# A conditioned two-matmul block on one core: the first LayerNorm, its shift and scale and the first weight loaded and applied in halves

## The chip, the cores and the metric

The kernel runs on one core of one Trainium2 chip. A core has a matrix engine (PE), a vector engine (DVE), a scalar engine (ACT), a general engine (POOL) and a queue engine (SP) that here only issues DMAs. Each engine works through its own list of instructions in order; they wait for one another by semaphores. The metric is the device time of one execution in microseconds (us), the median over runs.

## The reference

`x` is (2, 2048, 512) in float32, `t` (the condition) is (2, 512). All weights are float32.

```python
emb = jnp.dot(jax.nn.silu(t), ada_w) + ada_b
shift_msa, scale_msa, gate_msa, shift_mlp, scale_mlp, gate_mlp = jnp.split(emb, 6, axis=-1)
norm = _ln(x) * (1.0 + scale_msa[:, None]) + shift_msa[:, None]
h = jax.nn.gelu(jnp.dot(norm, ssm_w1) + ssm_b1, approximate=False)
ssm_out = jnp.dot(h, ssm_w2) + ssm_b2
x = x + gate_msa[:, None] * ssm_out
norm2 = _ln(x) * (1.0 + scale_mlp[:, None]) + shift_mlp[:, None]
hf = jax.nn.gelu(jnp.dot(norm2, ff_w1) + ff_b1, approximate=True)
ff_out = jnp.dot(hf, ff_w2) + ff_b2
x = x + gate_mlp[:, None] * ff_out
```

`_ln` is a LayerNorm without weights over the last axis. `ssm_w1` and `ssm_w2` are 512x512, `ff_w1` is 512x1024, `ff_w2` 1024x512. `ada_w` is 512x3072: six blocks of 512 columns, called groups 0 to 5 (0 and 1 are shift and scale of the first LayerNorm, 2 its gate, 3 and 4 shift and scale of the second, 5 its gate).

## The kernel before

The 4096 rows are cut into eight blocks of 512 rows. For each block four matrix stages run: `hA_i` (first LayerNorm's output times w1, GELU), `oA_i` (times w2, added to x), `hC_i` (second LayerNorm's output times ff_w1, GELU) and `oC_i` (times ff_w2, added to x). The order of all instructions is written out by hand: the program text is the order on every engine, and `hook` lists attach other engines' or later stages' work to a place "after product Pn" of a stage.

**Seven products.** A stage multiplies 2x2 quarters of its operands with seven products P1 to P7 instead of eight. `group` (L405) issues them on PE; each is four float32 matmuls of a 128x128 weight by 256 columns, and stands in the trace as eight records. The sums of quarters that the products need are made by other engines: those of the weight (`w_s`, by POOL, L340) and those of the activations (`nS` for a LayerNorm's output, `hSA` for a hidden stage's, by DVE, L340 too). The products accumulate in PSUM banks of three names, `y` (P1, then P6, P7, P4 on top of it), `x` (P2) and `v` (P5, then P3). So before P6 is added onto a bank `y`, an engine must have read what P1 left there; P7 waits in the same way for the reading of P6, P4 for that of P7, and P3 for that of P5.

In a hidden stage (`hidden`, L573) `after` reads the banks: P1, P6 and P5 are taken with the bias added (`take_first`: DVE, L594, or ACT in two halves if `on_act`, L592), P2, P7 and P3 are added to what was taken (DVE, L600, L607, L610) and pass through the GELU on ACT (L601, L608, L611); P4 goes through ACT alone (L614). In a residual stage (`residual`, L628) each product is added to x by DVE (L642).

**The first stages.** The rows of `t` and of the biases come by four small DMAs on ACT's queue. On SP's queue follow, in this order: x of block 0 (two halves), groups 0 and 1 of `ada_w`, w1, group 2, w2, the biases of the gate, b2, x of block 1, groups 3 and 4, ff_w1, group 5, ff_w2 and more. PE passes its first microseconds with matmuls of an identity that nobody reads (`idle`, L803), among them one that turns the rows (`rowsT`). DVE makes the statistics of the four 128-row slots of block 0 (`stats`, L454 and L455, one `mv` each), then copies the turned rows (`colsT`, L808), and ACT makes `silu` of them (L811). POOL and DVE turn the statistics into a scale and an offset per row (`scales`, L463 to L474; POOL's share is an addition and a power). ACT and DVE apply them (`normal`, L494 and L498, two slots each), PE turns the result (`pt`, L523, sixteen transposes in four banks), and ACT and DVE apply scale and shift per column while they move it from PSUM to SBUF (`modulate`, L537 and L539), which yields `nT`, the operand of `hA_0`.

Shift and scale come from `modulation(g0, part)`: `rows_of(g)` multiplies `silu` with a group of `ada_w` (`pada`, L267, sixteen small matmuls, 32 records), DVE turns the result (L283) and adds the bias (L287). The gate's rows come from `gate_rows_of` (the same matmuls, DVE L295), and `first_ssm_gate` spreads them over 128 partitions with four matmuls (`pgate`, L302). DVE then multiplies b2 with the gate (`gb`, L855) and folds the gate into the four parts of w2 (L388). POOL adds the product `gb` to x (`biases`, L654, four instructions) and makes the four sums of the folded w2 (`w_s`, L340).

Before the change the order of `hA_0` is P1, P2, group 2's rows, P5, `pgate`, P6, P3, P7, group 3's rows (`modulation(3, 0)`), P4. That of `oA_0` is P1, P2, P5, P6, group 4's rows (`modulation(3, 1)`), P7, P3, eight transposes of block 1, P4, eight more. DVE takes P1, P5 and P6 of `hA_0`.

Of the kernel before, what the change touches and what calls it, by code (L numbers as in the profile page):

```python
# [36 lines left out]
F32 = mybir.dt.float32  # L37
AF = mybir.ActivationFunctionType
ALU = mybir.AluOpType
# [101 lines left out]
def kernel(  # L141
# [52 lines left out]
    def big_tile(name):  # L194
        return big.tile([P, KD, D], F32, tag="big", name=name)
# [11 lines left out]
    def load_ada(g):  # L207
        ada[g] = big_tile(f"ada_{g}")
        nc.sync.dma_start(
            out=ada[g], in_=ada_w[:, g * D : (g + 1) * D].rearrange("(k p) n -> p k n", p=P)  # L210
        )

    def load_w(name, w, t=None, eng=nc.sync):
        if t is None:
            t = const.tile([P, w.shape[0] // P, w.shape[1]], F32, tag=name, name=name)
        eng.dma_start(out=t, in_=w.rearrange("(k p) n -> p k n", p=P))
        return t
# [16 lines left out]
    load_ada(0)  # L234
    load_ada(1)
    w1_sb = load_w("w1", w1)
# [22 lines left out]
    mods = {}  # L259
# [17 lines left out]

    def modulation(g0, part):

        g = g0 + part  # L280
        pa = rows_of(g)
        turned = pa[:, P : 2 * P]
        nc.vector.transpose(turned, pa[:, :P])  # L283
        turned = turned.rearrange("p (n q) -> p n q", n=KD)
        m = const.tile([P, KD, B], F32, tag=f"mod_{g0}_{part}", name=f"mod_{g0}_{part}")
        bias = colsT[:, R_ADA + g * KD : R_ADA + (g + 1) * KD]
        nc.vector.tensor_tensor(m, turned[:, :, :B], bias.unsqueeze(2).to_broadcast([P, KD, B]), ALU.add)  # L287
        mods[g0, part] = m

    gate, gate_rows = {}, {}  # L290
# [150 lines left out]
    class Norm:  # L441
# [40 lines left out]

        def blocks(self):
            return work.tile([P, C, KD, C, Q], F32, tag="blocks", name=f"blocks{self.name}")

        def normal(self, c, eng=None, on_pe=False):

            if c == 0:
                self.nT = big_tile(f"nT{self.name}")
                self.xn = self.blocks().rearrange("p m k c q -> p m (k c q)") if on_pe else self.nT  # L490
# [178 lines left out]
    hA_0 = forms[:, :8].rearrange("p n a r -> p (n a r)").rearrange("p (k t) -> p k t", k=KD)  # L669
# [137 lines left out]
    run(n1[0].stats())  # L807
    nc.vector.tensor_copy(colsT, pt[:, :ROWS])  # L808

# [5 lines left out]
    )  # L815

    for g in (1, 4):
        rows_g = colsT[:, R_ADA + g * KD : R_ADA + (g + 1) * KD]
        nc.vector.tensor_scalar(rows_g, rows_g, 1.0, None, ALU.add)

# [4 lines left out]
    n1[0].scales(on_dve=True)  # L825

    w1_ops, w1_sums, _ = weight_of_first("w1", w1_sb)
    run(w1_sums)
    modulation(0, 0)
    for c in range(C):  # L830
        n1[0].normal(c, nc.vector if c % 2 else None, on_pe=True)
    modulation(0, 1)
    pts = {}

    def transposed(k):
        pts[k] = n1[0].transpose(k, ps_g.tile([P, TB], F32, tag="yv"[k % 2], name=f"pt1_0_{k}"))

    for k in range(KD):
        transposed(k)
    for k in range(KD):  # L840
        n1[0].modulate(k, pts[k], nc.vector if k % 2 else None)
# [20 lines left out]
    hook(hooks, ("P2",), [lambda: gate_rows_of(2, "grows")] + n1_sums[3:])  # L862
    st = n1[1].stats()
    hook(hooks, ("P5",), [ssm_gate, gb2_0] + biases(0, b2_bc) + fold2(0, 1))
    hook(hooks, ("P6",), fold2(1, 7))
    hook(hooks, ("P3", "P7"), st[:2])
    hook(hooks, ("P7",), [lambda: modulation(3, 0)])
    hA[0] = First(0, n1[0].ops, hooks, ("P1", "P2", "P5", "P6", "P3", "P7", "P4"), hA_0)
# [7 lines left out]
    hook(hooks, ("P6",), [lambda: modulation(3, 1)])  # L876
    hook(hooks, ("P3", "P3", "P4"), n1[1].turned())
    n2 = {0: Norm(0, 2)}
# [268 lines left out]
```

## Time and profile before

| what | us |
|---|---|
| median of 5 runs | 597.76 |
| the five runs | 599.62, 597.76, 597.59, 597.76, 599.25 |
| the profiled execution, its own time | 599.62 |
| its span, first to last instruction | 597.8 |
| PE, DVE, ACT, POOL busy in it | 589.9, 373.0, 220.3, 394.2 |
| mean granted PE clock | 0.996 of full speed |

The profiled execution is the slowest of the five. The page gives busy times and the waits of each engine; the chain of waits follows the work that ended last back from the end; a table by stretches gives busy times and the clock that was granted to PE; the timeline lists the instructions of an engine in order of time, with start, duration, engine, line, operation, the tile written and the tiles read, and in brackets how long the engine sat idle before and what released it. "PEld" is PE's loading of weights, beside its matmuls.

### The profile page before, as it was taken

What the parts mean: (1) busy time and instruction counts of PE and PEld (TensorE: products, weight loads), DVE (VectorE), ACT (ScalarE), POOL (GpSimd) and SP (SyncE); (2) the same over time, 40 slices, a digit from 0 to 9 for tenths busy, and PEclk for the clock granted to TensorE, in tenths of its full rate; (3) what the DMA queues carried; (4) which work ended last, traced back from release to release, by engine and by line L of the source; (5) the groups of instructions that cost most, each with busy time, mean ns of one, the idle gap of its engine ahead of it and who ended that gap; (6) DMA issues with size and microseconds to landing.
All of it is one profiled execution on the core that took longest, in us unless ns stands there. A gap on an engine that the chain in (4) does not pass through costs nothing.

```text
span 597.8 us, 8294 instructions
## 1 busy us (share of the span) xinstructions
PE 589.9 (99%) x2875; PEld 511.7 (86%) x2875; DVE 373.0 (62%) x637; ACT 220.3 (37%) x366; POOL 394.2 (66%) x465
## 2 busy tenths in 40 slices
PE   7999999999999999999999999999999999999997
PEld 4888888888888888888888888888888888888886
DVE  4879898997654475655754458653665236468642
ACT  2234337305532264233721356232553234212410
POOL 1678489999943995549968499966974696440200
PEclk9999999999999999999999999999999999999999
DMA  8990322300223104350052601331030400021001
GB/s 317 396 377 4 89 63 80 107 36 35 63 80 106 53 1 107 135 146 1 15 145 66 208 9 42 100 72 70 1 70 2 115 27 2 0 67 76 1 1 71
DMA packets 23702, 50.13 MB, mean 84 GB/s; under 512 B 4544, under 2 KB 5100, under 8 KB 22764
## 3 DMA queue, kind: packets, MB, share of 16 engines
q1 hardware_dynamic: 20624, 45.38, 23.8%
q10 hardware_dynamic: 3036, 4.22, 3.0%
q8 instruction: 23, 0.38, 0.3%
q14 instruction: 19, 0.16, 0.1%
HBM read 26.51 MB, written 8.40 MB: 58 GB/s over the span
## 4 chain that ended last, share of the span: by engine, by line
PE 97%; DMA 2%; DVE 1%; SPq 0%; issue 0%
PE py_oC L420 18%; PE px_hC L741 10%; PE py_oA L420 9%; PE pv_oC L420 9%; PE py_hA L420 9%; PE py_hC L741 8%; PE pv_hC L741 8%; PE pv_oA L420 5%; PE px_oC L420 5%; PE pv_hA L420 4%; PE py_hC L420 2%; PE px_oA L420 2%; PE px_hA L420 2%; DMA ada<-in_L_cond_ada_w_dram 2%; PE pv_hC L420 1%; PE pt L523 1%
## 5 line engine op out<-in xcount | busy, mean ns | idle before, releaser
L654 POOL TENSOR_TENSOR x<-x,gb 128x512 f32<-128x512 f32 x64 | 79.4, 1272 | 7.8 <-issue 4.6
L537 ACT ACTIVATE nT<-nT,mod,mod 128x512 f32<-128x512 f32 x54 | 39.6, 802 | 102.4 <-DMA nT<-blocks 96.2
L463 POOL TENSOR_SCALAR ve<-mv 128x4 f32<-128x4 f32 x16 | 3.7, 230 | 92.3 <-DVE mv L455 85.5
L494 ACT ACTIVATE nT<-x,nmr,rstd 128x512 f32<-128x512 f32 x56 | 42.4, 803 | 52.9 <-POOL nmr L481 37.1
L420 PE MATMUL py_oC<-fw,hClo 128*128 128x256 f32 x256 | 57.9, 379 | 0.0
L420 PEld LDWEIGHTS py_oC<-fw,hClo 128*128 128x128 f32 x256 | 48.6, 190 | 6.6
L642 DVE TENSOR_TENSOR x<-py_oC,x 128x512 f32<-128x512 f32 (+1 forms) x36 | 22.6, 630 | 42.9 <-PE py_oC L420 42.9
L454 DVE BATCH_NORM_STATS2 st<-x 128x6 f32<-128x512 f32 x64 | 43.5, 679 | 5.1 <-DMA x<-in_x_dram 4.8
L340 POOL TENSOR_TENSOR hSC<-hClo,hChi 128x512 f32<-128x512 f32 (+1 forms) x17 | 20.1, 1187 | 39.9 <-ACT hChi L736 29.2
L741 PE MATMUL py_hC<-forms,fw 128*128 128x256 f32 x168 | 40.8, 379 | 0.0
L758 DVE TENSOR_TENSOR hClo<-hClo,py_hC 128x512 f32<-128x512 f32 x42 | 28.4, 681 | 16.9 <-ACT hClo L755 10.4
L505 DVE STREAM_TRANSPOSE blocks<-nT 128x512 f32<-128x512 f32 x56 | 37.8, 694 | 1.3 <-ACT nT L494 0.9
L679 POOL TENSOR_TENSOR forms<-forms 128x256 f32<-128x256 f32 x48 | 35.5, 740 | 2.8
L741 PEld LDWEIGHTS py_hC<-forms,fw 128*128 128x128 f32 x168 | 31.8, 190 | 4.4
L758 DVE TENSOR_TENSOR hChi<-hChi,pv_hC 128x512 f32<-128x512 f32 x35 | 23.3, 684 | 17.1 <-PE pv_hC L741 14.3
L642 DVE TENSOR_TENSOR x<-py_oA,x 128x512 f32<-128x512 f32 x32 | 22.0, 688 | 18.9 <-PE py_oA L420 18.3
L420 PE MATMUL py_hA<-nT,w 128*128 128x256 f32 x128 | 30.4, 380 | 0.0
L736 ACT ACTIVATE hClo<-hClo,colsT 128x256 f32<-128x256 f32 x56 | 25.4, 500 | 10.8 <-DVE hClo L758 10.7
L420 PE MATMUL py_oC<-fw_s,hSC 128*128 128x256 f32 x128 | 28.9, 379 | 0.0
L420 PE MATMUL pv_oC<-fw,hSC 128*128 128x256 f32 x128 | 28.9, 379 | 0.0
L420 PE MATMUL px_oC<-fw,hChi 128*128 128x256 f32 x128 | 28.9, 379 | 0.0
L420 PE MATMUL pv_oC<-fw_s,hSC 128*128 128x256 f32 x128 | 28.9, 379 | 0.0
(213 smaller groups left out, 1426.1 us busy)
## 6 DMA issues: line engine op xcount, KB each, us to landing
nT<-blocks SPq DMA_DIRECT2D x168, 64.0 KB
out_dram<-x SPq DMA_DIRECT2D x15, 512.0 KB
x<-in_x_dram SPq DMA_DIRECT2D x7, 1024.0 KB
ada<-in_L_cond_ada_w_dram SPq DMA_DIRECT2D x6, 1024.0 KB
fw<-in_L_cond_ff_w_dram SPq DMA_DIRECT2D x3, 2048.0 KB
nT<-blocks ACTq DMA_DIRECT2D x56, 64.0 KB
w<-in_L_cond_ssm_w_dram SPq DMA_DIRECT2D x3, 1024.0 KB
x<-in_x_dram SPq DMA_DIRECT2D x2, 512.0 KB
```

The lines of the kernel that those rows point to most:

```text
L340: eng.tensor_tensor(out[:, r], a[:, r], b[:, r], f)
L420: nc.tensor.matmul(ps[b][j * apart][:, j, :], lhs(p, j, k), rhs(p, j, k), start=(fresh and j * (not apart) == 0 and k == 0), stop=(p in (" ...
L454: nc.vector.bn_stats(st, xs[self.i][:, c, :])
L494: nc.scalar.activation(t, x_c, AF.Identity, bias=self.nmr[:, c : c + 1], scale=self.rstd[:, c : c + 1])
L505: nc.vector.transpose(self.bl[:, :, :, c, :].rearrange("p m k q -> p k m q"), self.nT[:, c, :].rearrange("p (k m q) -> p k m q", k=KD, m=C),)
L537: nc.scalar.activation(dst, src, AF.Identity, bias=shift, scale=scale)
L642: nc.vector.tensor_tensor(d, ps[BANK[p]][:, js], d, ALU.add)
L654: lambda c=c: nc.gpsimd.tensor_tensor(xs[i][:, c, :], xs[i][:, c, :], gb, ALU.add)
L679: eng.tensor_tensor(reg[d], reg[a], reg[b], ALU.add if f == "+" else ALU.subtract)
L736: nc.scalar.activation(h, h, AF.Gelu_apprx_tanh, bias=fb1T[:, m : m + 1])
L741: nc.tensor.matmul(ps[b][:, j, :], fa[ra][:, j * P : (j + 1) * P], fb[rb].rearrange("p a (c q) -> p c a q", q=Q), start=(fresh and j == 0) ...
L758: nc.vector.tensor_tensor(dest(d), dest(d), ps[b], op)
```

## The change

Shift and scale (groups 0 and 1) and w1 are loaded in two halves of their columns each, in the order shift low, scale low, shift high, scale high, w1 low, w1 high: six DMAs with rows of 1 KB where there were three with rows of 2 KB. `modulation` works on one half at a time and gives back its DVE part as a function (`finish`). The scales of the first LayerNorm are made for slots 0 and 1 and for slots 2 and 3 apart (`scales_of`); ACT normalizes slots 0 and 1, DVE slots 2 and 3. The transposes come as slots 0 and 1 of all four banks, then slots 2 and 3, between the rows of the low and the high halves. `nT` of block 0 lies in the second half of `forms` instead of a tile of the pool `big`.

In `hA_0` ACT takes P1, P5 and P6 (`on_act=True`), and the order is P1, P2, P5, group 2's rows, P6, `pgate`, P7, P3, P4. In `oA_0` group 3's rows stand between P6 and P7, and group 4's after P4 and the last transposes. The four statistics of block 1 (`st`) stand after P3, P4 of `hA_0` and, as before, after P1 of `oA_0`; `picks` is made later.

```diff
@@ -204,10 +204,12 @@
 
     ada = {}
 
-    def load_ada(g):
-        ada[g] = big_tile(f"ada_{g}")
+    def load_ada(g, half=None):
+        if not half:
+            ada[g] = big_tile(f"ada_{g}")
+        c = slice(0, D) if half is None else slice(half * D // 2, (half + 1) * D // 2)
         nc.sync.dma_start(
-            out=ada[g], in_=ada_w[:, g * D : (g + 1) * D].rearrange("(k p) n -> p k n", p=P)
+            out=ada[g][:, :, c], in_=ada_w[:, g * D : (g + 1) * D][:, c].rearrange("(k p) n -> p k n", p=P)
         )
 
     def load_w(name, w, t=None, eng=nc.sync):
@@ -231,9 +233,12 @@
     ident = const.tile([P, P], F32, tag="ident", name="ident")
     make_identity(nc, ident)
     load_x(0, 2)
-    load_ada(0)
-    load_ada(1)
-    w1_sb = load_w("w1", w1)
+    for half in range(2):
+        load_ada(0, half)
+        load_ada(1, half)
+    w1_sb = const.tile([P, KD, D], F32, tag="w1", name="w1")
+    for c in (slice(0, D // 2), slice(D // 2, D)):
+        nc.sync.dma_start(out=w1_sb[:, :, c], in_=w1[:, c].rearrange("(k p) n -> p k n", p=P))
     load_ada(2)
 
     nc.gpsimd.memset(brows[:, :2, :P], 0.0)
@@ -256,7 +261,45 @@
     load_ada(4)
     fw1_sb = load_w("fw1", fw1)
 
-    mods = {}
+    mods, pada = {}, {}
+
+    def modulation(g0, part, half=None):
+
+
+        g = g0 + part
+        if not half:
+            pada[g] = ps_g.tile([P, D], F32, tag="x", name=f"pada_{g}")
+            mods[g0, part] = const.tile([P, KD, B], F32, tag=f"mod_{g0}_{part}", name=f"mod_{g0}_{part}")
+        n = slice(0, KD) if half is None else slice(half * KD // 2, (half + 1) * KD // 2)
+        pa = pada[g][:, n.start * G : n.stop * G]
+        w = ada[g].rearrange("p k (n m q) -> p k m n q", n=KD, q=G)
+        for k in range(KD):
+            for m in range(P // G):
+                nc.tensor.matmul(
+                    pa[m * G : (m + 1) * G, :],
+                    silu[:, k, :],
+                    w[:, k, m, n],
+                    start=(k == 0),
+                    stop=(k == KD - 1),
+                    tile_position=(0, m * G),
+                    skip_group_check=True,
+                )
+        turned = pada[g][:, P + n.start * G : P + n.stop * G]
+        bias = colsT[:, R_ADA + g * KD : R_ADA + (g + 1) * KD][:, n]
+
+        def finish():
+            nc.vector.transpose(turned, pa)
+            to = mods[g0, part][:, n]
+            by_n = turned.rearrange("p (n q) -> p n q", q=G)
+            nc.vector.tensor_tensor(
+                to, by_n[:, :, :B], bias.unsqueeze(2).to_broadcast([P, n.stop - n.start, B]), ALU.add
+            )
+
+        if half is not None:
+            return finish
+        finish()
+
+    gate, gate_rows = {}, {}
 
     def rows_of(g):
 
@@ -274,20 +317,6 @@
                     skip_group_check=True,
                 )
         return pa
-
-    def modulation(g0, part):
-
-        g = g0 + part
-        pa = rows_of(g)
-        turned = pa[:, P : 2 * P]
-        nc.vector.transpose(turned, pa[:, :P])
-        turned = turned.rearrange("p (n q) -> p n q", n=KD)
-        m = const.tile([P, KD, B], F32, tag=f"mod_{g0}_{part}", name=f"mod_{g0}_{part}")
-        bias = colsT[:, R_ADA + g * KD : R_ADA + (g + 1) * KD]
-        nc.vector.tensor_tensor(m, turned[:, :, :B], bias.unsqueeze(2).to_broadcast([P, KD, B]), ALU.add)
-        mods[g0, part] = m
-
-    gate, gate_rows = {}, {}
 
     def gate_rows_of(g, tag):
         pa = rows_of(g)
@@ -480,13 +509,33 @@
             v.tensor_tensor(self.nmr, self.mv[:, :, 0], self.rstd, ALU.mult)
             v.tensor_scalar(self.nmr, self.nmr, -1.0, None, ALU.mult)
 
+        def scales_of(self, s):
+
+            n, v = f"{self.name}_{s.start}", nc.vector
+            if s.start == 0:
+                self.rstd = small.tile([P, C], F32, tag="rstd", name=f"rstd{self.name}")
+                self.nmr = small.tile([P, C], F32, tag="nmr", name=f"nmr{self.name}")
+            ve, r, e = [small.tile([P, C], F32, tag=k, name=f"{k}{n}")[:, s] for k in ("ve", "r", "e")]
+            nc.gpsimd.tensor_scalar(ve, self.mv[:, s, 1], EPS, None, ALU.add)
+            nc.gpsimd.tensor_tensor(r, ve, minus_half[:, s], ALU.pow)
+
+            def rest():
+                v.tensor_tensor(e, r, ve, ALU.mult)
+                v.scalar_tensor_tensor(e, e, -0.5, r, ALU.mult, ALU.mult)
+                v.scalar_tensor_tensor(self.rstd[:, s], e, 1.5, r, ALU.add, ALU.mult)
+                v.scalar_tensor_tensor(
+                    self.nmr[:, s], self.mv[:, s, 0], -1.0, self.rstd[:, s], ALU.mult, ALU.mult
+                )
+
+            return rest
+
         def blocks(self):
             return work.tile([P, C, KD, C, Q], F32, tag="blocks", name=f"blocks{self.name}")
 
         def normal(self, c, eng=None, on_pe=False):
 
             if c == 0:
-                self.nT = big_tile(f"nT{self.name}")
+                self.nT = nT_0 if self.name == "1_0" else big_tile(f"nT{self.name}")
                 self.xn = self.blocks().rearrange("p m k c q -> p m (k c q)") if on_pe else self.nT
             t = self.xn[:, c, :]
             x_c = xs[self.i][:, c, :]
@@ -666,7 +715,10 @@
 
     forms = const.tile([P, 16, C, HT // C], F32, tag="forms", name="forms")
 
-    hA_0 = forms[:, :8].rearrange("p n a r -> p (n a r)").rearrange("p (k t) -> p k t", k=KD)
+    hA_0, nT_0 = [
+        forms[:, n : n + 8].rearrange("p n a r -> p (n a r)").rearrange("p (k t) -> p k t", k=KD)
+        for n in (0, 8)
+    ]
 
     def sums_of_registers(program, reg, engs):
 
@@ -804,8 +856,14 @@
             idle, ident, ident.unsqueeze(1).to_broadcast([P, C, P]), start=True, stop=True
         )
 
-    run(n1[0].stats())
+    halves = slice(0, C // 2), slice(C // 2, C)
+    st = n1[0].stats()
+    run(st[:2])
+    scales_lo = n1[0].scales_of(halves[0])
+    run(st[2:])
     nc.vector.tensor_copy(colsT, pt[:, :ROWS])
+    scales_hi = n1[0].scales_of(halves[1])
+    scales_lo()
 
 
     nc.scalar.activation(
@@ -813,32 +871,42 @@
         colsT[:, R_COND:R_ADA].rearrange("p (b k) -> p b k", b=B),
         AF.Silu,
     )
+    for c in (0, 1):
+        n1[0].normal(c, on_pe=True)
 
     for g in (1, 4):
         rows_g = colsT[:, R_ADA + g * KD : R_ADA + (g + 1) * KD]
         nc.vector.tensor_scalar(rows_g, rows_g, 1.0, None, ALU.add)
+    scales_hi()
+    for c in (2, 3):
+        n1[0].normal(c, nc.vector, on_pe=True)
+    w1_ops, w1_sums, _ = weight_of_first("w1", w1_sb)
+    run(w1_sums)
+
+
+    pts = {k: ps_g.tile([P, TB], F32, tag="yv"[k % 2], name=f"pt1_0_{k}") for k in range(KD)}
+
+    def transposed(k, slots):
+        for c in slots:
+            nc.tensor.transpose(pts[k][:, c * P : (c + 1) * P], n1[0].xn[:, c, k * P : (k + 1) * P], ident)
+
+    for finish in [modulation(0, part, 0) for part in range(2)]:
+        finish()
+    for k in range(KD):
+        transposed(k, (0, 1))
+    for k in range(KD):
+        transposed(k, (2, 3))
+    n1[0].modulate(0, pts[0])
+    n1[0].modulate(1, pts[1], nc.vector)
 
     picks = const.tile([P, P // G, P], F32, tag="picks", name="picks")
     nc.vector.tensor_copy(
         picks, ident.rearrange("p (m q) -> p m q", q=G)[:, :, :1].to_broadcast([P, P // G, P])
     )
-    n1[0].scales(on_dve=True)
-
-    w1_ops, w1_sums, _ = weight_of_first("w1", w1_sb)
-    run(w1_sums)
-    modulation(0, 0)
-    for c in range(C):
-        n1[0].normal(c, nc.vector if c % 2 else None, on_pe=True)
-    modulation(0, 1)
-    pts = {}
-
-    def transposed(k):
-        pts[k] = n1[0].transpose(k, ps_g.tile([P, TB], F32, tag="yv"[k % 2], name=f"pt1_0_{k}"))
-
-    for k in range(KD):
-        transposed(k)
-    for k in range(KD):
-        n1[0].modulate(k, pts[k], nc.vector if k % 2 else None)
+    for finish in [modulation(0, part, 1) for part in range(2)]:
+        finish()
+    n1[0].modulate(2, pts[2])
+    n1[0].modulate(3, pts[3], nc.vector)
     n1_sums = n1[0].summed(nc.vector)
     run(n1_sums[:2])
     load_ada(5)
@@ -859,13 +927,13 @@
 
     hooks = {}
     hook(hooks, ("P1",), n1_sums[2:3])
-    hook(hooks, ("P2",), [lambda: gate_rows_of(2, "grows")] + n1_sums[3:])
+    hook(hooks, ("P2",), n1_sums[3:])
     st = n1[1].stats()
-    hook(hooks, ("P5",), [ssm_gate, gb2_0] + biases(0, b2_bc) + fold2(0, 1))
-    hook(hooks, ("P6",), fold2(1, 7))
-    hook(hooks, ("P3", "P7"), st[:2])
-    hook(hooks, ("P7",), [lambda: modulation(3, 0)])
-    hA[0] = First(0, n1[0].ops, hooks, ("P1", "P2", "P5", "P6", "P3", "P7", "P4"), hA_0)
+    hook(hooks, ("P5",), [lambda: gate_rows_of(2, "grows")])
+    hook(hooks, ("P6",), [ssm_gate, gb2_0] + biases(0, b2_bc) + fold2(0, 1))
+    hook(hooks, ("P7",), fold2(1, 7))
+    hook(hooks, ("P3", "P4"), st[:2])
+    hA[0] = First(0, n1[0].ops, hooks, FIRST, hA_0, on_act=True)
     w2_ops = found["w2"][0]
 
     hA_sums = hA[0].summed(nc.vector)
@@ -873,8 +941,9 @@
     hooks = {}
     hook(hooks, ("P1",), hA_sums[2:3] + st[2:] + [n1[1].scales] + fold2(7, 8))
     hook(hooks, ("P2",), hA_sums[3:] + [lambda c=c: n1[1].normal(c, on_pe=True) for c in range(C)])
-    hook(hooks, ("P6",), [lambda: modulation(3, 1)])
+    hook(hooks, ("P6",), [lambda: modulation(3, 0)])
     hook(hooks, ("P3", "P3", "P4"), n1[1].turned())
+    hook(hooks, ("P4",), [lambda: modulation(3, 1)])
     n2 = {0: Norm(0, 2)}
     st = n2[0].stats()
     hook(hooks, ("P3",), st[:2])
```

## The prediction

> **What bounds the kernel now.** The page first: its busy times, and the shares of the chain that ended last.
>
> ```profile
> PE 589.9 (99%) x2875; PEld 511.7 (86%) x2875; DVE 373.0 (62%) x637; ACT 220.3 (37%) x366; POOL 394.2 (66%) x465
> PE 97%; DMA 2%; DVE 1%; SPq 0%; issue 0%
> ```
>
> PE is the bound. The change leaves the number of products alone, so it can only gain where PE waits or runs slowly. The chain in order of time (start, length, what) shows where that is:
>
> ```profile
> 2.11 9.84 DMA ada<-in_L_cond_ada_w_dram
> 11.99 1.58 PE pada L267 x32
> 13.57 3.01 PE pt L523 x16
> 16.58 1.73 PE py_hA L420 x8
> ```
>
> Until 11.99 us the end is set by the loads of shift and scale; from the first product of `hA_0` (first matmul at 16.42) PE goes from product to product at 1.73 each. What stands ahead of 16.42 can be shortened, nothing else. Then the table by stretches (length, busy time of each engine, granted PE clock, DMA):
>
> ```profile
> 5.59:9.00 3.41, 2.80 (x7) 0.81 (x5) 3.14 (x11) 0.22 (x1) 0.62 (x2) 1.00 1.03 385
> 9.00:12.42 3.42, 1.51 (x48) 1.27 (x52) 1.98 (x8) 1.52 (x2) 0.80 (x1) 1.00 1.04 390
> 12.42:15.83 3.41, 3.41 (x35) 3.03 (x28) 0.81 (x3) 0.78 (x1) 1.10 (x1) 0.50 1.04 387
> 31.00:40.00 9.00, 9.00 (x71) 7.68 (x69) 8.79 (x15) 0.84 (x2) 5.06 (x9) 1.00 1.04 389
> ```
>
> Two readings. After a stretch of 3.4 us in which PE was busy for 1.51, the clock was 0.50 for the next 3.41: sixteen transposes took 3.01 where eight take 0.87 in the chain at 43.87, and `pada` 1.58 instead of 1.08. That is 1.27 + 0.50 = 1.8 us of this execution, and the five times lie in two groups just so far apart (597.6 to 597.8; 599.25 and 599.62). The profiled one, 599.62, paid it; the median run, 1.86 below, did not. And from 31 to 40 us DVE is busy 8.79 of 9.00: beside PE there is no slack in `oA_0`. Its timeline, with PE's and POOL's lines:
>
> ```profile
> 31.15 1.27 POOL L340 TENSOR_TENSOR w_s<-w,w_s 128x512 f32<-128x512 f32 x1
> 31.40 1.57 DVE L340 TENSOR_TENSOR hSA<-forms 128x512 f32<-128x512 f32 x1
> 32.38 1.72 POOL L340 TENSOR_TENSOR w<-w 128x512 f32<-128x512 f32 x1
> 33.01 1.64 DVE L340 TENSOR_TENSOR hSA<-hSA,forms 128x512 f32<-128x512 f32 x1
> 37.32 1.89 PE L420 MATMUL py_oA<-w_s,hSA 128*128 128x256 f32 x8
> 37.95 0.68 DVE L340 TENSOR_TENSOR hSA<-forms,hSA 128x512 f32<-128x512 f32 x1
> 39.14 1.08 PE L267 MATMUL pada<-ada,silu 128*32 128x128 f32 x32
> 39.24 0.69 DVE L642 TENSOR_TENSOR x<-py_oA,x 128x512 f32<-128x512 f32 x1
> 40.15 1.99 PE L420 MATMUL py_oA<-w,forms 128*128 128x256 f32 x8
> ```
>
> DVE's addition of P6 ends at 39.93, group 4's rows cover that time on PE, and P7, which reuses P6's bank, starts at 40.15. It just fits. A sum `hSA` costs 0.68 alone and 1.6 while POOL makes sums of its own.
>
> **The change, part by part (us).**
>
> *Loads.* 1 MB of `ada_w` takes 2.65 (9.37 to 11.99; group 0 thus begins near 6.7). The halves have rows of 1 KB. The trace's packets of 1,024 bytes, the closing stores, took 48 ns, those of 2,048 bytes 88 at 9 to 15 us: two for one is 1.09 times as long, 1.46 a half. Landings: shift low 8.15, scale low 9.6, shift high 11.1, scale high 12.55, w1 low 14.0, w1 high 15.45. Bounds: no loss (w1 low 13.4) and 1 KB slowed as 2 KB was at 5.5 us, 97 for 88 (14.6). Three more DMAs cost SP three issues of 0.4 to 0.6, under loads already queued. Everything behind w1 lands some 0.8 later: w2 near 21.7 for its first use after 24, block 1's x near 25 for statistics at 28.5. Free; without that cover, 0.8.
>
> *LayerNorm in halves.* Statistics of slots 0 and 1 end at 6.47; POOL's 0.25 + 1.18 is done at 8.0. DVE's four small operations (0.20 each) follow `colsT` (8.29): 9.1. ACT's two normals (0.76 each) end at 9.9 and 10.65. The second half: POOL 8.29 to 9.8, DVE to 10.65, two normals of 0.5 to 11.6. Before, the last ended at 12.14.
>
> *PE until P1.* `silu` stays at 8.61. Half a group is 16 matmuls of 64 columns: between half of 1.08 and all of it; I take 0.87, since 32 weight loads alone took 0.81. Low halves 8.65 to 9.5 and 9.6 to 10.5; eight transposes (0.87) 10.7 to 11.55; eight more from 11.65 to 12.5; high halves to 13.4 and 14.25. Low shift and scale are ready at 12.4, the two modulations (0.8) at 13.3; the high ones at 14.85 and 15.65, before P2's turn at 16.0. So P1 starts at 14.25 (w1 low: 14.05) instead of 16.42: -2.17. Of this 1.8 is the slow clock that PE, now hardly idle, should avoid; against the median run only some 0.35 is left. Bounds: 13.6 (cheap half groups, full-rate loads) to 14.9.
>
> *ACT takes P1, P5 and P6.* DVE loses three operations of 0.60 spacing, ACT gains three of 0.84 (L614's pair) and has room (0.84 busy in nine). P6 stands ahead of `pgate` (1.04), which hides ACT's reading of it from P7, up to 0.1; uncovered 1.0.
>
> *Group 2's rows and `pgate` one product later.* Here the gain is given back. From P1 to the end of `pgate`: four products 6.92, rows 1.2 (19.93 to 21.13 with both gaps), `pgate` 1.04: 9.2, so DVE's `gb` starts at P1 + 9.4, 23.7. Before it was P1 + 7.6. The DVE work freed lies ahead of this wait and doesn't help. From there to the end of P6's addition in `oA_0`, by starts: `gb` 0.6, first fold 0.6, wait for P7 0.6, its addition 0.6, three folds 1.8, P3's addition 0.6, two statistics 1.6, two `hSA` 3.2, addition 0.6, sum 0.6, two statistics 1.6, P2's addition, `hSA`, P5's addition 1.8, P6's 0.7: 14.9, end at 38.6. PE from P1 to P7 of `oA_0`: eleven products 19.0, rows 2 x 1.2, `pgate` 1.04, the 0.1: 22.55, at 36.8. P7 must wait for the bank: 1.8; with 0.05 of signalling +1.85. Bounds: if the two `hSA` miss POOL's sums they cost 1.8 less and the stall is nil; if the sum behind them is caught too (POOL's three begin at 29.4, DVE's at 30.1), +0.5.
>
> *Groups 3 and 4.* The same 1.2 each, later; that group 3's rows left `hA_0` is in PE's sum above. DVE's part of group 4 (0.5) comes ahead of block 1's sums, ready at 49.4 for a product at 50.3. Nothing.
>
> *Sum* against the profiled execution's own time: 599.62 - 2.17 + 1.85 = **599.3**. This is 0.26% above the median before, whose runs had the first 1.8 already. A measurement can tell 0.3% from no change, here 1.8 us.
>
> [...] The row first: 1.51 busy of 3.42, with gaps of 0.4 and 1.54, was followed by half clock. [...]
>
> **The rivals.**
>
> *A, the forecast* (599.3; own range 598.6 to 600.0).
>
> *B, the stall brings the slow clock.* PE at P7 of `oA_0` is idle for 1.85, so a stretch of 3.41 that holds it whole has PE busy 1.56, like the 1.51 above; 2.80 kept the clock. If so the next 3.41 run at half: + 1.7, 601.0, slower than before. It decides where the stall lies wholly in one stretch: (3.41 - 1.85) / 3.41, 46% of the positions, which seem to shift from run to run. Against it: the least busy time that keeps the clock lies anywhere between 1.51 and 2.80.
>
> *C, no stall.* DVE gets by POOL, and P7 doesn't wait: 599.62 - 2.17 = 597.45, with an early P1 596.8. For it: three operations fewer on DVE. Against it: the wait for `pgate` comes after them.
>
> *D, the halves don't land earlier.* Rows of 1 KB need 60 ns or the slow clock falls on the transposes as before: P1 at 15.9, 599.62 - 0.5 + 1.85 = 601.0. Against it: 48 ns in the records, and gaps of 0.2 where there were 1.54.
>
> **How the numbers follow.** A 0.45, B 0.19, C 0.28, D 0.08. Before's median is 597.76, so "within 0.3%" is 595.97 to 599.55. Faster: a part of C, 0.11. Same: the rest of C and two thirds of A, 0.48. Slower: a third of A, B and D, 0.41. The predicted time is A's, 599.3; the range reaches from C's early end to B, 596.9 to 601.1.
>
> **What would show it.** Right: P1's first matmul at 14.0 to 14.6; clock 1.00 from 9 to 16 us; ACT with three pairs on L641; a gap of some 1.9 on PE ahead of the third `py_oA` product of `oA_0`, released by DVE's addition, with `hSA` at 1.1 to 1.7 beside POOL's sums. Wrong: no gap there; a clock of 0.50 near 40 us (B) or 12 us (D); half groups of `pada` over 1.1. The largest doubt is whether POOL's sums meet DVE's.

## The result, and the profile after

The changed kernel takes 599.34 us (median of 31 runs, 598.96 to 600.74) against 597.8 before (56 runs). The ratio is 1.002, with a 95% interval of 1.0015 to 1.0025: a little slower, 1.2 us by the ratio and 1.5 by the medians. The forecast was 599.3. The profiled execution of the kernel after took 599.35, with a span of 597.6. (In what follows PE is also called TensorE, DVE VectorE, ACT ScalarE, POOL GpSimd and SP SyncE.)

First the page of the kernel after: busy times, and shares of the chain that ended last.

```profile
PE 588.8 (99%) x2939; PEld 511.0 (86%) x2939; DVE 370.1 (62%) x642; ACT 222.7 (37%) x372; POOL 395.8 (66%) x467
PE 90%; DVE 4%; POOL 2%; DMA 2%; issue 1%; ACT 0%; ACTq 0%; DVEq 0%
```

PE fell from 97% of the chain to 90, and VectorE's share rose from 1 to 4: the chain no longer runs through PE alone. PE's timeline of the kernel after has three waits of over half a us once `hA_0` begins (start, length, what, and in brackets the idle time before it with its releaser):

```profile
14.10 1.97 PE L449 MATMUL py_hA<-forms,w 128*128 128x256 f32 x8 [0.79 <-DMA w<-in_L_cond_ssm_w_dram]
...
38.49 1.97 PE L449 MATMUL py_oA<-w,forms 128*128 128x256 f32 x8 [1.67 <-DVE x L691]
...
76.64 1.97 PE L449 MATMUL py_hC<-nS,fw_s 128*128 128x256 f32 x8 [0.88 <-DVE hClo L643]
```

The first line is the gain: P1 of `hA_0` at 14.10. The second is the forecast's stall, P7 of `oA_0` waiting for VectorE's addition of P6. The third was not foreseen. VectorE's lines ahead of the stall:

```profile
21.34 0.29 DVE L324 TENSOR_TENSOR grows<-pada,brows 128x128 f32<-128x128 f32 x1 [1.89 <-DMA brows<-in_L_cond_ada_b_dram]
23.43 0.69 DVE L923 TENSOR_TENSOR gb<-pgate,gb 128x512 f32<-128x512 f32 x1 [1.80 <-PE pgate L331]
...
25.55 0.69 DVE L656 TENSOR_TENSOR forms<-py_hA,forms 128x512 f32<-128x512 f32 x1 [0.83 <-PE py_hA L449]
...
30.16 0.84 DVE L369 TENSOR_TENSOR hSA<-forms 128x512 f32<-128x512 f32 x1
31.03 1.64 DVE L369 TENSOR_TENSOR hSA<-hSA,forms 128x512 f32<-128x512 f32 x1
...
33.20 1.15 DVE L369 TENSOR_TENSOR forms<-forms 128x512 f32<-128x512 f32 x1
...
37.66 0.68 DVE L691 TENSOR_TENSOR x<-py_oA,x 128x512 f32<-128x512 f32 x1
```

VectorE stands idle for 1.9 and 1.8 us before `gb`, and for 0.83 more until P7 of `hA_0` can be read; from there it has no pause, and sums that take 0.68 beside none of GpSimd's (36.46) take up to 1.64 beside one (31.03; GpSimd's from 30.53 to 32.13). Last, the stretches of the forecast, and one of the same length that holds the stall whole (length, busy time of each engine, granted clock, DMA):

```profile
5.59:9.00 3.41, 3.22 (x35) 1.23 (x37) 3.17 (x14) 0.36 (x2) 1.71 (x4) 1.00 1.06 357
9.00:12.42 3.42, 3.14 (x81) 2.53 (x73) 2.85 (x11) 1.94 (x3) 0.20 (x1) 1.00 1.09 349
12.42:15.83 3.41, 2.62 (x72) 2.31 (x63) 3.20 (x9) 0.99 (x2) 0.30 (x1) 1.00 1.09 361
36.39:39.81 3.42, 1.75 (x22) 1.38 (x15) 2.35 (x6) 0.64 (x1) 2.93 (x8) 1.00 1.05 387
```

The clock stays at 1.00 in all of them, also where PE is busy for only 1.75 of 3.42.

### The profile page after: what moved, and what is told of

It reads as the page before. It is cut to its first block, busy times and chain, and to the rows that moved or that the text cites. A ratio compares the mean times of both kernels' runs of the same rounds, so it can differ in the third digit from the quotient of the medians.

```text
span 597.6 us, 8442 instructions
## 1 busy us (share of the span) xinstructions
PE 588.8 (99%) x2939; PEld 511.0 (86%) x2939; DVE 370.1 (62%) x642; ACT 222.7 (37%) x372; POOL 395.8 (66%) x467
## 3 DMA queue, kind: packets, MB, share of 16 engines
q1 hardware_dynamic: 22208, 45.38, 24.4%
## 4 chain that ended last, share of the span: by engine, by line
PE 90%; DVE 4%; POOL 2%; DMA 2%; issue 1%; ACT 0%; ACTq 0%; DVEq 0%
PE py_oC L449 18%; PE px_hC L793 10%; PE pv_oC L449 9%; PE py_hA L449 9%; PE py_hC L793 8%; PE pv_hC L793 8%; PE py_oA L449 8%; PE px_oC L449 5%; PE pv_hA L449 4%; PE pv_oA L449 4%; PE px_hA L449 2%; PE px_oA L449 2%; PE py_hC L449 1%; DMA w<-in_L_cond_ssm_w_dram 1%; POOL x L703 1%; DVE x L691 1%
## 5 line engine op out<-in xcount | busy, mean ns | idle before, releaser
L449 PE MATMUL py_oC<-fw_s,hChi 128*128 128x256 f32 x128 | 28.9, 379 | 0.0
```

The lines of the kernel that those rows point to most:

```text
L449: nc.tensor.matmul(ps[b][j * apart][:, j, :], lhs(p, j, k), rhs(p, j, k), start=(fresh and j * (not apart) == 0 and k == 0), stop=(p in (" ...
```

## The experiments

All times are medians; the ratio is to the kernel before on the same chip, with its 95% interval. "P1" is the first matmul of `hA_0`, "P7" the idle time ahead of P7 of `oA_0`, "others" PE's further idle times from P1 on to 100 us, those of 0.15 and more; all from the profiled execution (us).

| kernel | us | ratio | P1 | P7 | others |
|---|---|---|---|---|---|
| before, second profile | 597.62 | | 14.71 | 0 | none |
| after | 599.34 | 1.002 [1.0015, 1.0025] | 14.10 | 1.67 | `hC_0` P6 0.88 |
| moves alone | 599.73 | 1.0027 [1.0017, 1.0037] | 14.80 | 1.64 | `hC_0` P6 0.15 |
| halves alone | 598.51 | 1.0011 [1.0002, 1.002] | 14.11 | 0 | `pada_2` 1.85 |
| gate early | 600.15 | 1.0034 [1.0022, 1.0047] | 14.12 | 0 | `pada_2` 1.30, `hA_0` P4 0.78, `hC_0` P6 0.68 |
| no collision | 597.71 | 0.9995 [0.9985, 1.0004] | 15.57 | 0 | `hC_0` P6 0.52 |
| last sum late | 599.48 | 1.0015 [1.0004, 1.0025] | 14.14 | 1.08 | transposes 0.38, `hC_0` P6 0.76 |
| gate amid P6 | 599.57 | 1.002 [1.001, 1.0029] | 14.00 | 1.01 | `hA_0` P7 0.98, `hC_0` P6 0.49 |
| three together | 598.80 | 1.001 [1.0, 1.002] | 14.28 | 0.46 | `hA_0` P7 0.98, transposes 0.38, `hC_0` P4 0.39 |
| order of before | 598.19 | 1.0001 [0.9992, 1.001] | 14.18 | 0 | `pada_3` 1.17, `oA_0` P3 0.34, `hC_0` P4 0.56 |
| sum back | 597.75 | 0.9996 [0.9988, 1.0005] | 14.56 | 0 | `pada_3` 0.84, `hC_0` P4 0.38 |
| ScalarE alone | 597.69 | 0.9998 [0.9987, 1.0008] | 16.36 | 0 | none |
| rows in time | 597.14 | 0.998 [0.9971, 0.999] | 14.16 | 1.05 | none |

**A second profile of before** (no edit).

> The kernel before, unchanged, for a second profile of it. The page of before showed 3.41 us at half clock (12.42 to 15.83), which costs 1.7 us, and its runs lie in two groups 1.7 apart. Theory: the half clock is a matter of single executions; in an execution without it P1 of hA_0 starts 1.7 earlier, at about 14.7 instead of 16.42, and the time is 597.8; in one with it 599.5. Rival: the two groups come from elsewhere (a load that lands late), and P1 starts at 16.4 in both. Also looked for: whether P6 of hC_0, at about 75, has a gap before it; theory (the gate's way through DRAM made the 0.9 gap in the kernel after): below 0.2.

It took 597.62, and its stretches are these:

```profile
5.59:9.00 3.41, 3.41 (x7) 1.11 (x5) 3.17 (x11) 0.21 (x1) 0.69 (x2) 1.00 1.03 393
9.00:12.42 3.42, 1.71 (x53) 1.36 (x56) 1.96 (x8) 1.52 (x2) 0.80 (x1) 1.00 1.05 389
12.42:15.83 3.41, 3.41 (x43) 3.08 (x34) 2.22 (x5) 2.11 (x3) 1.21 (x1) 1.00 1.05 386
```

The clock stays at 1.00 in all three, and P1 starts at 14.71, 1.71 earlier than 16.42. The middle row must not be set beside the 1.51 of the profile shown first. In the profile shown first the granted clock changed at 12.42, 15.83 and 596.10, which is 2, 3 and 173 times 3.413 after 5.59, where its record of the clock begins; here the first step is at 7.06. Between steps counted from there PE is busy for longer:

```profile
7.06:10.47 3.41, 3.13 (x37) 1.28 (x35) 2.27 (x12) 0.21 (x1) 1.49 (x2) 1.00 1.05 398
10.47:13.88 3.41, 1.98 (x41) 1.78 (x42) 1.93 (x7) 1.74 (x3) 0.00 (x0) 1.00 1.05 386
```

Here 1.98 was followed by a clock of 1.00, in the profile shown first 1.51 by one of 0.50. The two groups of times of before are this half clock: of the 96 runs of before made beside the experiments, the 19 with a mean granted clock of 0.997 or less took 599.0 to 600.5; the other 77 have a median of 597.76, and only one of them took over 599.0. So the change wins 0.61 at P1, not 2.3, against an execution such as this. It is the right one to compare with:

```profile
35.52 1.89 PE L420 MATMUL py_oA<-w_s,hSA 128*128 128x256 f32 x8
37.34 1.08 PE L267 MATMUL pada<-ada,silu 128*32 128x128 f32 x32
38.35 2.00 PE L420 MATMUL py_oA<-w,forms 128*128 128x256 f32 x8
```

P7 of `oA_0` starts at 38.35 here and at 38.49 after, and VectorE's addition of P6 ends at 38.13 here (37.44 + 0.69) and at 38.34 after (37.66 + 0.68). VectorE sets this point in the kernel after, and in before it was only 0.2 from doing so. Counted from P1, VectorE's addition ends 0.82 later than here (24.24 against 23.42), and TensorE is ready for P7 0.93 sooner (22.71 against 23.64), since group 4's rows no longer stand ahead of it: the wait of 1.67 is made of both. At that point the kernel after still owes 1.0 of group 4's rows, which before had behind it: P1 of `hA_1` follows at 46.59 against 45.38, 1.21 later.

**The parts of the change, one at a time.** "Moves alone" has the hooks, the order of products and ScalarE's reading of after in the kernel before; "halves alone" the opposite (a part of its edit, against after):

```
-    hA[0] = First(0, n1[0].ops, hooks, FIRST, hA_0, on_act=True)
+    hook(hooks, ("P2",), [lambda: gate_rows_of(2, "grows")] + n1_sums[3:])
...
+    hA[0] = First(0, n1[0].ops, hooks, ("P1", "P2", "P5", "P6", "P3", "P7", "P4"), hA_0)
```

> Before, with the moved rows of the gate and of the second shift and ScalarE's reading of block 0's first product, but with whole loads and an undivided LayerNorm. Theory (the later gate is the loss): P1 of hA_0 at 14.7 to 15.0 (no half clock), gb nine and a half after it, P7 of oA_0 waits 1.7 to 1.9 for P6's addition, and the time is 597.8 + 1.7 - 0.2 = 599.3, ratio 1.0025. Rival (the halved loads, which make group 2 land 2.0 later, are the loss): no stall by it, 597.6 to 597.8, ratio 1.000.

> After, with the hooks of before: VectorE takes every first product, the gate's rows stay behind P2 and the second shift's behind P7. Theory: P1 starts at 14.1, no stall at oA_0's P7, but the gate's rows, due at 17.6, wait for group 2's landing at 19.4: 1.8 us on TensorE, of which 0.6 is what the earlier P1 had won: 597.8 + 1.2 = 599.0, ratio 1.002. Rival (the halves cost nothing, only the later gate does): 597.8 - 0.6 = 597.2, ratio 0.999.

The moves alone give the stall (1.64) without the early P1, and are the slowest of the three. So the stall needs no halves. The halves alone have no stall at `oA_0`, but another wait:

```profile
15.91 1.89 PE L449 MATMUL px_hA<-forms,w 128*128 128x256 f32 x8
19.65 1.08 PE L310 MATMUL pada<-ada,silu 128*32 128x128 f32 x32 [1.85 <-DMA ada<-in_L_cond_ada_w_dram]
```

With the rows still behind P2, PE waits for group 2's landing. Both parts lose by themselves (medians: moves +2.0, halves +0.8), and together they lose less than their sum (+1.5), since rows one product later no longer wait for that landing. The rival that only the loads were at fault falls with the first kernel, the one that they cost nothing with the second.

> After, with the gate's rows behind P2 and the gate behind P5 as before, in the order of products of before; halves, ScalarE's reading and the two later groups of rows stay as after. Theory: as the halves alone, TensorE waits 1.8 us for group 2's landing, and ScalarE's reading changes less than 0.2: 599.0, ratio 1.002. Rival (only the later gate is the loss): 597.2, ratio 0.999.

"Gate early" is after with the gate's hooks as in the diff above but ScalarE's reading kept, and group 3's rows left in `oA_0`. Both expectations missed: 600.15. The wait at `pada_2` came, with 1.30 instead of the 1.8 foreseen; what neither had is this:

```profile
29.27 1.99 PE L449 MATMUL py_hA<-nS,w 128*128 128x256 f32 x8 [0.78 <-DVE forms L656]
```

P4 uses the bank that VectorE has just read P7 from. In before, group 3's rows stand between the two products and cover that reading; here they are gone. The group of rows between these two products of one bank was a cover, and moving it uncovers 0.78.

> Before, with nothing but ScalarE's reading of P1, P5 and P6 of hA_0. Theory (this part costs nothing, the moved rows cost all): 597.8, ratio 0.9995 to 1.0005. Rival (ScalarE's reading, 0.84 in two instructions in place of VectorE's 0.60, delays P6 or P7 in bank y): a gap of 0.3 to 0.9 before them, 598.1 to 598.7.

"ScalarE alone" (`on_act=True` in before, nothing else): 597.69, nothing, as the theory has it. Its profiled execution had the half clock again, from 12.30 on; the step before it:

```profile
8.89:12.30 3.41, 1.45 (x46) 1.21 (x50) 1.96 (x8) 1.52 (x2) 0.87 (x1) 1.00 1.03 382
```

**What makes the stall as long as it is.**

```
-    hook(hooks, ("P7",), fold2(1, 7))
+    hook(hooks, ("P7",), fold2(1, 4))
...
+    for j in range(2):
+        nc.gpsimd.memset(w2_s[:, j], 0.01)
```

> After, without GpSimd's first three sums of the folded w2 (two of the summed tiles are filled with a constant earlier, and the third sum, in place in w2, is left out), so that these sums lie beside no sum of VectorE's. Theory (the shared access of the two engines sets the size of the stall): VectorE's three sums of hSA and forms take 0.68 each in place of 0.84, 1.64 and 1.15, that is 1.6 less in the chain before P6's addition, and the wait of oA_0's P7 falls from 1.67 to 0 to 0.2: 599.34 - 1.5 = 597.8. Rival (the chain from pgate alone sets it, and the sums' length is other waiting): wait 1.2 or more, 598.9 to 599.3.

```profile
31.59 0.66 DVE L369 TENSOR_TENSOR hSA<-forms 128x512 f32<-128x512 f32 x1
32.28 0.69 DVE L369 TENSOR_TENSOR hSA<-hSA,forms 128x512 f32<-128x512 f32 x1
...
33.49 0.68 DVE L369 TENSOR_TENSOR forms<-forms 128x512 f32<-128x512 f32 x1
```

These are the three sums of after's second fence of VectorE, now 0.66 to 0.69 each: 1.60 less in all. The wait is gone and the time is 597.71, 1.63 less than after. In this profiled execution the first loads landed some 1.5 late (w1's low half at 15.45 instead of 13.98, hence P1 at 15.57), so starts are to be read as distances: from P1 to the end of P6's addition VectorE needs 22.59 (38.16 - 15.57), after 24.24 (38.34 - 14.10). What GpSimd's sums add to VectorE's, 1.60, is thus worth the whole stall. The change did not bring it: in the second profile of before the same three sums take 1.58, 1.64 and 0.67, and nothing waits. It takes both, the moves and GpSimd's sums.

```
-    hook(hooks, ("P2",), hA_sums[3:] + [lambda c=c: n1[1].normal(c, on_pe=True) for c in range(C)])
-    hook(hooks, ("P6",), [lambda: modulation(3, 0)])
+    hook(hooks, ("P2",), [lambda c=c: n1[1].normal(c, on_pe=True) for c in range(C)])
+    hook(hooks, ("P6",), [lambda: modulation(3, 0)] + hA_sums[3:])
```

> After, with the last sum of hSA moved behind P6's addition (it is used at P3, 1.9 after P7's start). Theory (VectorE's work in order sets P7's start): one instruction of 0.60 less before the addition, wait 1.07 in place of 1.67, 599.34 - 0.6 = 598.7. Rival (VectorE only waits there for something else, such as TensorE's P5 or P6): wait unchanged, 599.3.

The wait fell by just the 0.6 foreseen, to 1.08, but the time did not (599.48). The sum now starts at 38.30, in the time of GpSimd's small operations for block 1's LayerNorm; ScalarE's normals, which wait for the last of these (`nmr`), start at 39.69 instead of 39.17, and the transposes wait for them, 0.38 in one piece; from the first of the eight to P4 it is 1.67 (41.61 to 43.28) instead of 0.87 (42.02 to 42.89):

```profile
42.68 0.76 PE L572 MATMUL pt<-ident,blocks 128*128 128x128 f32 x5 [0.38 <-ACT blocks L543]
```

```
-    hook(hooks, ("P6",), [ssm_gate, gb2_0] + biases(0, b2_bc) + fold2(0, 1))
+    hook(hooks, (("P6", 0),), [ssm_gate, gb2_0] + biases(0, b2_bc))
+    hook(hooks, ("P6",), fold2(0, 1))
...
                 if apart:
                     after(p, {b: ps[b][j]}, slice(j, j + 1))
+                for op in hooks.get((p, j), ()):
+                    op()
```

> After, with the products of the gate by the picks put between the two halves of P6 of hA_0 instead of behind it, and the gate's bias rows loaded before w2 instead of behind it (they are what the rows' addition waited for). Theory (the later gate is the loss): gb starts 0.8 to 0.9 earlier (22.6 instead of 23.43), and the stall of oA_0's P7 is smaller by as much, 0.8 in place of 1.67: 598.5. Rival (the collision with GpSimd's sums goes along with the folds and takes it back, or w2 lands too late for the fold): wait 1.3 or more, 599.0 to 599.3.

(Of this edit, the new order of the loads is not shown.) `gb` started at 22.77, 0.66 earlier, and the wait fell by 0.66, to 1.01. That the two numbers agree is an accident:

```profile
23.40 0.84 ACT L642 ACTIVATE forms<-py_hA,colsT 128x256 f32<-128x256 f32 x2 [2.50 <-PE py_hA L448]
24.34 0.89 PE L448 MATMUL py_hA<-forms,w 128*128 128x256 f32 x3 [0.98 <-issue]
...
26.41 0.69 DVE L657 TENSOR_TENSOR forms<-py_hA,forms 128x512 f32<-128x512 f32 x1 [2.36 <-PE py_hA L448]
...
37.87 0.68 DVE L692 TENSOR_TENSOR x<-py_oA,x 128x512 f32<-128x512 f32 x1
```

VectorE's addition of P6 ended at 38.55, later than in the kernel after (38.34): what `gb` had won, VectorE spent waiting for P7 of `hA_0`, 2.36 instead of 0.83. The wait of `oA_0`'s P7 is shorter because PE came to it 0.87 later (37.68 against 36.81), while VectorE's way from the reading of P7 to the end of the addition was 0.65 shorter (12.14 against 12.79): its three sums met less of GpSimd's and took 0.66, 1.64 and 0.67. So this kernel does not show that the gate's lateness is the loss. The time was no better (599.57), and neither theory had why: P7 of `hA_0`, next in P6's bank, now waited 0.98. The trace names no releaser, but ScalarE's reading of P6, which `pgate` behind P6 had covered, ends at 24.24, just ahead of it.

**Towards a better version.** With the last sum late, the gate amid P6, and the second gate's product and folds moved later as well (only this last part is shown):

```
-    hook(hooks, ("P7",), [gb5_0] + n2_sums[1:] + [lambda c=c: n1[2].normal(c) for c in range(C)] + gb5)
-    hook(hooks, ("P7", "P3", "P4"), fold5(0, 3))
+    hook(hooks, ("P7",), n2_sums[1:] + [lambda c=c: n1[2].normal(c) for c in range(C)])
+    hook(hooks, ("P3",), [gb5_0] + gb5)
+    hook(hooks, ("P4",), fold5(0, 1))
```

> The gate between the halves of P6 with the early bias rows, the last sum of hSA behind P6's addition, and, third, the product of the second gate and its folds one to three products later, so that VectorE reads hC_0's first product before it would wait for the gate's way through DRAM. Theory: wait of oA_0's P7 0.2 in place of 1.67, gap before hC_0's P6 0.0 in place of 0.9 (0.1 to 0.9 over executions), P1 of hA_0 at 14.1: 599.34 - 1.45 - 0.5 = 597.4, ratio to before 0.9994. Rival (the waits come back elsewhere, at the pieces moved later): 598.3 or more.

598.80. The gap before `hC_0`'s P6 is gone and the stall is 0.46, but the 0.98 and the 0.38 of the last two kernels came along. Next, group 3's rows went back between P7 and P4, group 4's behind `oA_0`'s P6, and P3 between P6 and P7 (the lines added in `hA_0`):

```
+    hook(hooks, ("P6", "P6", "P3", "P3", "P7"), fold2(0, 7))
+    hook(hooks, ("P7", "P4"), st[:2])
+    hook(hooks, ("P7",), [lambda: modulation(3, 0)])
+    hA[0] = First(0, n1[0].ops, hooks, ("P1", "P2", "P5", "P6", "P3", "P7", "P4"), hA_0, on_act=True)
```

> The kernel of the three changes together (gate between the halves of P6, last sum of hSA late, second gate's product late), and with the order of products of before for hA_0: the second shift's rows again between P7 and P4 of hA_0, the second scale's behind P6 of oA_0, P3 behind the divided P6. Theory (rows or the gate between two products of one bank hide the reading of that bank; the 0.98 at P7 of hA_0 in the last two kernels was ScalarE's reading of P6 left bare): no gap in hA_0, P7 of oA_0 waits 0 to 0.4, no gap before hC_0's P6; TensorE 0.2 to 0.5 earlier than in the kernel before, and 597.0 to 597.5, ratio 0.9987 to 0.9996. Rival (the gap of 0.98 is TensorE's own, by the divided product, and comes back; VectorE is again late by a us): 598.3 or more.

> The same with the last sum of hSA where before and after have it, ahead of P6's addition. Theory: 0.6 more on VectorE ahead of P7 of oA_0, whose wait is 0.4 to 1.0, less 0.38 at the transposes of block 1, which in the kernels with the late sum waited for the normals: 0.2 more than the last, 597.2 to 597.8. Rival (VectorE has that slack): the same as the last or 0.4 less.

The 0.98 is gone with the order, although P6 is still divided; so it was the reading of P6's bank, and not the division. In its place group 3's rows wait for their weights, 1.17 in the one and 0.84 in the other: P7 of `hA_0` is over before group 3 lands. With the sum back in its place the kernel is 0.44 faster, not 0.2 slower (the rival is right): moved, it took 1.69 instead of 0.68 and held up P3 of `oA_0` for 0.34. Last, group 3 is loaded ahead of block 1's x, and two folds go to the next group:

```
-    load_x(1)
+    xs[1] = big_tile("x_1")
     load_ada(3)
+    nc.sync.dma_start(out=xs[1], in_=x_blk[1])
...
-    hook(hooks, ("P6", "P5", "P5", "P7", "P7", "P3", "P4"), fold5(1, 8))
+    hook(hooks, ("P6", "P5", "P7", "P3", "P4"), fold5(1, 6))
```

> The kernel with the sum back, with two waits that its trace shows taken out: group 3 is loaded ahead of x_1 (its rows in hA_0 waited 0.84 for the landing), and two of the second gate's folds go one group later (hC_0's P4 waited 0.38 behind VectorE's folds). Theory (each gap on TensorE before the steady loop costs its length): 0.84 + 0.38 less on TensorE, x_1's statistics start at about 28 as now: 597.75 - 1.2 = 596.6, ratio to before 0.998. Rival (x_1, now 3 us later, holds up the statistics and with them VectorE's sums of hSA, and P7 of oA_0 waits instead): 597.2 to 597.8.

```profile
14.16 1.97 PE L449 MATMUL py_hA<-forms,w 128*128 128x256 f32 x8 [0.77 <-DMA w<-in_L_cond_ssm_w_dram]
38.77 1.97 PE L449 MATMUL py_oA<-w,forms 128*128 128x256 f32 x8 [1.05 <-DVE x L693]
```

597.14, ratio 0.998 [0.9971, 0.999]: it beats both kernels, by half of what was expected. Both waits are gone, and one is back: PE now reaches P7 of `oA_0` sooner, and VectorE's addition of P6 ends at 38.62 (37.94 + 0.68), as it did in the kernel with the sum back (38.76). What is won ahead of that point on PE alone ends there. Nor is the 0.6 gained on before TensorE's: VectorE's last addition of all starts at 591.97 here and at 591.92 in the second profile of before. What is shorter is the time behind it, 3.33 against 3.88, which the next section takes up.

## Why the forecast was right, point by point

*P1 of `hA_0`* was put at 14.25 and came at 14.10. Two terms were mis-sized and nearly cancel: a half group took 0.55, not 0.87, but w1's low half landed at 13.98 all the same, and P1 waited 0.79 for it. The packets of 1 KB took 51 ns instead of 48 (350 GB/s over 16 engines is 47 ns for each, at a busy share of 1.10; before: 389 GB/s and 1.05, 88 ns for 2 KB). That 1.8 of the gain was the half clock of one execution is shown by the second profile of before (1.71).

*"Everything behind w1 lands some 0.8 later. Free; without that cover, 0.8."* Free was right, since the rows had been moved; the size was not. By SP's next issues, which wait for the landings, w1 landed 0.8 later than in the profile shown first (15.47 against 14.67) and group 2 2.0 later (19.38 against 17.38), and without the cover it cost 1.85 (halves alone). Why group 2 lost another 1.2, at 381 to 384 GB/s, is open.

*ScalarE's reading* costs nothing, and P6's is hidden by `pgate` ("uncovered 1.0"): no gap over 0.1 in the kernel after and, uncovered, 0.98.

*The stall.* The forecast had `gb` at 23.7, the end of P6's addition at 38.6, PE ready at 36.8 and 1.85 lost; the trace has 23.43, 38.34, 36.81 and 1.67. Place and size are right, and that VectorE's work in order makes it is shown: one sum of 0.6 less shortens it by 0.6, GpSimd's sums away by all of it; the moves alone bring it. That it starts from `gb` is not: the chain's "wait for P7" (0.6 in the forecast, 0.83 in the trace) ties it to TensorE again, and VectorE works without a pause only from the reading of P7 of `hA_0` on, 12.79 up to the end of the addition. With `gb` 0.66 earlier the addition ended no sooner. Which of the moves makes VectorE's 0.82 was not tried apart. No run shows the 0.05 of signalling; from 38.34 to P7's start at 38.49 it is 0.15. The two sums of `hSA` and the one behind them were to take 3.8 and took 3.5 by their starts.

*Groups 3 and 4.* Their rows meet no wait where the change puts them, as forecast; but group 4's 1.0, which in before ran while VectorE finished, now follows the wait. That their places are covers for a bank's reading (0.78, 0.98) was not in the forecast.

*Two terms were missing, of opposite sign.* The first is the gap before `hC_0`'s P6. VectorE reads `hC_0`'s first product late, since the second gate's product ahead of it in its queue waits for ScalarE's copy:

```profile
71.60 0.59 ACT L357 COPY pgate<-gsb 128x512 f32<-128x512 f32 x1 [1.65 <-DMA gsb<-gates]
```

The copy waits for the gate's way through DRAM. SP issued the load at 68.37, 1.95 after the last of the four stores (63.77 + 2.65); in the profile of before shown first it was 1.09 (68.03 - 66.94), in the second, with moves alone and with halves alone 1.1. Against the second profile of before, P1 of `hC_0` is 1.09 late and P6 2.13. The second is at the end: from the start of the last addition to the end of the span it is 3.39 (597.6 - 594.21) where before has 3.88 (595.8 - 591.92); in halves alone 3.28, in moves alone 3.86. Against the execution the forecast started from, the last addition starts 0.27 later (594.21 against 593.94) and the span 0.2 shorter. So that the sum came out at 599.3 is luck: the gap adds 0.88, the end takes back 0.47, and P1 and the stall were 0.15 and 0.18 better than foreseen.

The traces also show where the end is won. SyncE closes the program with five waits, in the same order in both kernels, each for two of the semaphores that the DMAs signal. The last three stores signal 101, 102 and 103 in before and 104, 105 and 106 in after, three on, as there are three DMAs more. In before 103 stands in the first wait, so all five pass only after the last store has signalled it (596.27): they pass from 596.28 to 596.57, and the span ends at 597.82. In after 106 stands in the fourth wait: the first three are over before the store lands (595.04 to 595.18, landing 596.62), the other two pass at 596.64 and 596.72, and the span ends at 597.56. From the last packet of the last store to the end it is 2.07 in before (from 595.75) and 1.55 in after (from 596.01). Of this half a us the order of the waits shows 0.2 (0.08 between the first and the last that pass after the landing, against 0.29). Behind the fifth wait it is 0.84 against 1.25 to the end, and what makes that 0.4 was not tried; the landing itself comes 0.61 behind the last packet, against 0.52. The 0.8 that halves alone loses has such a gain in it (3.28 against 3.88).

*The rivals.* B (the stall brings the half clock) did not happen: 1.75 busy of 3.42, from 36.39, nine steps after 5.67, where after's record of the clock begins, was followed by 1.00. Its longest gap was 1.67; the rows of 1.51 and 1.45, whose longest gaps were 1.54, were followed by 0.50. C (no stall) is what GpSimd's sums decide, as the forecast said: without them 597.71, where C had 597.45. D (late halves) falls with P1 at 14.10.

## What to carry to other kernels

Where two engines run side by side, look for the point that the second one sets, and at how far it is from the first: here VectorE's addition ended 0.2 before TensorE needed it, so no more than that of what was won on TensorE alone could get past this point, and work taken off VectorE ahead of it (0.6, 1.6) shortened TensorE's wait by as much. When two numbers agree, follow both engines all the same: in "gate amid P6" the wait shrank by just what `gb` had won, and for another reason. Work that stands between two uses of one bank was here also the cover for reading it (0.78 and 0.98); before moving it, name what covers the reading next. And compare with an execution that lacks the accidents of the one profiled: three quarters of the apparent gain here was a half clock that most runs never had.

## What the runs showed of the hardware

- The granted clock changed at 12.42, 15.83 and 596.10 in the profile of before shown first, and fell at 12.30 in that of "ScalarE alone". It was 0.50 after a step of 3.41 us with PE busy for 1.51 (9.00 to 12.42) and for 1.45 (8.89 to 12.30), and 1.00 after one with 1.98 (second profile of before, 10.47 to 13.88) and one with 1.75 (after, 36.39 to 39.81). The longest single gap inside these steps was 1.54 in the first two, 1.43 and 1.67 in the others: in these four the busy time told them apart and the gap did not.
- A sum of VectorE's with both operands in SBUF took up to 1.76 us (after, at 16.00) beside a sum of GpSimd's (15.53 to 17.22) instead of 0.68 (after, at 14.61, GpSimd idle). The three ahead of the stall, 0.84, 1.64 and 1.15 in after, took 0.66 to 0.69 with GpSimd's sums away (no collision). It goes both ways: the first of GpSimd's sums of w1 took 1.69 there (after, 15.53), and 1.27 in before (14.72), where it met no sum of VectorE's. What in the hardware makes it so was not tried.
- The closing stretch, from the last addition to the end of the span, was 3.39 in after (597.6 - 594.21) and 3.86 in before (597.8 - 593.94). In after three of the five closing waits were over before the last store landed, in before none; the waits explain 0.2 of the difference.
- The load behind the four stores of the second gate (1 KB each) was issued 1.09 us after the last of them in before (68.03 against 66.94) and 1.95 after it in after (68.37 against 66.42). In after two fetches of 8 KB on the instructions' queue (q14 on the page) begin in that time, at 67.17 and 68.31; in before the first begins at 68.78, when the load has been issued. Whether the fetch holds up the load was not tried.
